# Loads through one queue in order of use, keys turned after the values' second product, and the maxima split for both query blocks at once

## The chip, the cores and the metric

The program runs on one core of a Trainium2 chip. The time is that of one execution on the device, in microseconds (us); the number compared is the median of several runs. A core has a matrix engine (PE, with its weight loads, PEld, shown beside it), a vector engine (DVE), a scalar engine (ACT), a general engine (POOL) and a sequencer (SP) that issues transfers. Each engine works through its own instructions in order; transfers run on 16 shared DMA engines, fed from a queue of SP and a queue of ACT.

## The reference

Eight sequences of 256 rows and 512 columns go through four residual steps, each with a layer norm in front and the tanh of a gate as factor. Cut to what matters here:

```python
x = x + tanh(g_xattn[0]) * causal_attention(layernorm(x), ctx, ctx)     # 16 heads of 32, keys = values = context
x = x + tanh(g_ffn[0])   * ternary_ffn(layernorm(x))                    # weights quantized per group of 64, in bf16
x = x + tanh(g_xattn[1]) * cross_attention(layernorm(x), ctx)           # q, k, v, o linears; q and k normed by their rms
x = x + tanh(g_ffn[1])   * bit_ffn(layernorm(x))                        # 8-bit activations, ternary weights
```

The second attention takes its keys and values from the context through `k_img_w` and `v_img_w`: `k = rms_norm(ctx @ k_w.T + k_b)`, `v = ctx @ v_w.T + v_b`. They don't depend on x. Both attentions need a maximum per query row and head before their exponentials.

## The kernel before

The work is in three stages. In the first (lines 819 to 861) the kernel quantizes the weights of the first feed-forward, computes the keys and values of the second attention for all eight sequences and parks them in device memory, and does the first attention of the sequences 0 and 1. In the second (1123 to 1162) PE runs the first feed-forward of all sequences, with the other attentions between its chunks. In the third (1365 to 1391) it runs the second feed-forward with the remaining cross attentions.

**The written order.** Each piece of work is a step with a place on a time axis, and `timeline` (617) emits the steps in order of their places. In the first stage one unit of the axis is one unit of weights (a block of 128 x 1024), and three units go with one sequence's keys and values. PE keeps this order exactly, since `pe.held` chains its instructions (860). The other engines and the queues don't: the framework orders their instructions by its own estimate of when each becomes ready, earlier places first among those that are ready, and adds the waits. `behind` (301) pins an instruction after a named one.

**A unit u of weights** (`quantize0`, 701): `sizes` at u - 0.5 starts the load of unit u + 1 and has ACT write the absolute values `a` and the signs `sg` (716); `mean(0)` at u is a product on PE into the one bank of `mean`, copied out by ACT into `s` (724); `rest` at u + 0.45 is the second such product and five instructions of DVE (736 to 740). The loads of units go into two buffers, so unit 2 can only be loaded when the signs of unit 0 are done.

**A sequence b of keys and values** (`keys_values`, 790): `load` of the turned context `cT`; `k0` and `k1`, two linears of eight records on PE, each with the bias `rkb` added by DVE and squared by ACT (756, 757); `scale`, where POOL takes the root (274) and scales the two halves (764); `turn`, eight transposes on PE into a pair of banks and a copy of 1024 columns by ACT (348); `store` of the keys (803); `v0` and `v1`, the values' linears with the bias `rvb` (810), the second followed by the store of the values (812). Its places within the three units are in lines 845 to 849: k0 0.1 (for sequence 0 at -0.6), k1 0.85, scale 0.9, v0 1.6, turn 2.15, store 2.16, v1 2.35.

**The first attention of sequences 0 and 1** (850 to 857) has its steps at 0.5, 1.25 and 2.75 of each three units: the turn of its queries `y` (569), four `scores` (385), whose row maxima `nm` are reduced by DVE (412), then `parts` (423), `shift` (443), four `exps` (451) and four `weigh` (488). `parts` splits each maximum into three bf16 terms in the tile `mz`, in POOL: per query block q and term k a copy that rounds and, but for the last term, a subtraction, ten instructions on 16 values per partition. `shift` turns `mz` on PE (tile `nt`, 447) and DVE copies it to `nT` (449), which `exps` uses as an operand. `scores`, `exps` and `turned` share the two pairs of banks of tag `s`.

**The first loads** (826 to 834): SP issues `cT` of sequence 0, units 0 and 1, `wv` (1 MB) and the rows x0 and x1; ACT issues the gates, the four blocks of `wk` and the broadcast rows `rkb` and `rvb`, before its first computations. Behind these SP issues, in the order that the framework chose, the first attentions' `kT` and `v`, the next `cT`, x2 and x3, and unit 2.

**Into the second stage**: the rows x4 to x15 are loaded into a pool that takes the place of the first stage's buffers, so these loads wait until the tiles beneath are free. Sequence 2's layer norm (`norm`, 563) reads x4 and x5; `layernorm` pins its DVE statistics (281) behind the last product with the up half that was emitted before it (912). Its place is 1.4 of the first 16 chunks (line 1153), between chunks 1 and 2; its turn is at 4.2. A chunk is `hidden` (892): 32 products into a bank `gu`, of which there are two, then ACT's tanh, two DVE instructions (911, 912), a cast and a subtraction for the low half; `project` (927) follows three chunks later.

Of the kernel before, what the change touches and what calls it, by code (L numbers as in the profile page):

```python
# [45 lines left out]
ALU = mybir.AluOpType  # L46
# [4 lines left out]
P = 128  # L51
# [26 lines left out]
MP = 3  # L78
# [9 lines left out]
def flamingo_kernel(  # L88
# [273 lines left out]
    class Attention:  # L362
# [60 lines left out]
        def parts(self):  # L423

            part = self.mz.rearrange("p q (r k g) -> p k r q g", r=4, g=DC)
            rest = small.tile([P, 4, 2, DC], F32, tag="nmr", name="nmr", bufs=2)
            src = self.nm
            for k in range(MP):
                for q in range(2):
                    if k + 1 < MP:  # L430
                        nc.gpsimd.tensor_scalar(
                            part[:, k, :, q], src[:, :, q], 1.0, 0.0, ALU.mult, ALU.add
                        )
                        nc.gpsimd.tensor_tensor(
                            rest[:, :, q], src[:, :, q], part[:, k, :, q], ALU.subtract
                        )
                    else:
                        nc.gpsimd.tensor_scalar(
                            part[:, k, :, q], src[:, :, q], 1.0, 0.0, ALU.mult, ALU.add
                        )  # L440
                src = rest

        def shift(self):
# [163 lines left out]
    def load_w(pool, name, wT):  # L607
        w = pool.tile([P, DC, D], F32, tag=f"w{name}", name=f"w{name}", bufs=1)
        nc.sync.dma_start(out=w, in_=wT.rearrange("(c p) o -> p c o", p=P))
        return w  # L610

    def load_row(pool, name, row, tag=None, bufs=1):
        t = pool.tile([P, D], F32, tag=tag or f"r{name}", name=f"r{name}", bufs=bufs)
        nc.scalar.dma_start(out=t, in_=row.partition_broadcast(P))
        return t

    def timeline(*jobs):
# [202 lines left out]
    with ExitStack() as part:  # L820
# [4 lines left out]
        wk = [prep.tile([P, D], F32, tag=f"wk{c}", name=f"wk{c}") for c in range(DC)]  # L825
        kv[0][0]()
        for c in range(DC):
            nc.scalar.dma_start(out=wk[c], in_=k_wT[c * P : (c + 1) * P, :])
        for u in range(AHEAD + 1):
            load0(u, prep)  # L830
        rkb, rvb = load_row(prep, "kb", k_b), load_row(prep, "vb", v_b)
        wv = load_w(prep, "v", v_wT)
        load_x(0, x0)
        load_x(1, x0)

# [5 lines left out]
        for b in range(B):  # L841
            load, k0, k1, scale, turn, store, v0, v1 = kv[b]
            if b:
                jobs += on((3 * b - 2, load))
            jobs += on(
                *((3 * b + n, f) for n, f in zip(
                    (0.1 if b else -0.6, 0.85, 0.9, 2.15, 2.16, 1.6, 2.35), (k0, k1, scale, turn, store, v0, v1)
                ))
            )
        for a, n in zip(att0, (0, 12)):  # L850
            places = [n + 3 * k + f for k in range(5) for f in (0.5, 1.25, 2.75)]
            jobs += on(*zip((n + 0.3, n + 0.35, places[2]), a.ready()))
# [270 lines left out]
    with ExitStack() as part:  # L1123
# [320 lines left out]
```

## Time and profile before

| | |
|---|---|
| median of 3 runs | 1199.13 us (1198.99 to 1200.08) |
| the profiled execution's own time | 1195.64 us |
| its span, first to last instruction | 1193.9 us |
| PE busy | 1091.6 us (91%) |
| DVE busy | 789.3 us (66%) |
| ACT busy | 595.2 us (50%) |
| POOL busy | 503.2 us (42%) |
| granted PE clock, mean | 0.987 |

Times in the profile count from the first instruction. The first stage runs to about 196 us. A linear of 512 columns shows as eight records of 0.43 us; PE's ends are modelled, so waits are read from the idle time that stands in brackets before an instruction, with what ended it. A broad share of the whole says little here, since the stages have different limits; the rows of the stretch in question do.

### The profile page before, as it was taken

The numbers are of one execution on the slowest core, as the hardware profiler recorded it, in microseconds if no ns is written. First come the engines' busy times: TensorE is split into PE (matmuls) and PEld (weight loads), VectorE is DVE, ScalarE is ACT, GpSimd is POOL, SyncE is SP. The second block draws the span as 40 slices with busy tenths as digits, with TensorE's granted clock in tenths as the row PEclk, the third lists the DMA queues.
The fourth block names the chain that finished last, engine by engine and source line by source line (L and its number), as shares of the span: only waits on it lengthen the run. The fifth ranks groups of instructions, "written<-read, shape, count | busy, mean of one in ns | idle before, by whom it ended". The sixth has DMA issues, their size and how long they took to land.

```text
span 1193.9 us, 31314 instructions
## 1 busy us (share of the span) xinstructions
PE 1091.6 (91%) x13290; PEld 737.9 (62%) x13389; DVE 789.3 (66%) x1612; ACT 595.2 (50%) x1058; POOL 503.2 (42%) x794
## 2 busy tenths in 40 slices
PE   5899998999999988988899998898999999999986
PEld 1445446777777666766677776565656565656653
DVE  5786986745546374655646445786868686868586
ACT  3566554565665443344344442546364636464663
POOL 3113013433435474575544326544444444424251
PEclk9999999999999999999999999999999999999999
DMA  8444436423333232333211014012121212211212
GB/s 299 144 171 150 168 112 209 129 92 120 97 123 81 86 83 89 100 89 103 64 49 42 19 37 159 18 47 51 49 50 50 49 50 50 54 32 32 42 39 59
DMA packets 99469, 104.08 MB, mean 87 GB/s; under 512 B 60992, under 2 KB 72320, under 8 KB 99328
## 3 DMA queue, kind: packets, MB, share of 16 engines
q1 hardware_dynamic: 95728, 96.03, 27.4%
q10 hardware_dynamic: 3600, 6.03, 1.5%
q8 instruction: 105, 1.72, 0.6%
q14 instruction: 36, 0.29, 0.1%
HBM read 72.09 MB, written 15.73 MB: 74 GB/s over the span
## 4 chain that ended last, share of the span: by engine, by line
PE 35%; DVE 30%; POOL 15%; ACT 11%; issue 7%; DMA 3%; DVEq 0%; SPq 0%; POOLq 0%; ACTq 0%
PE gu L257 9%; PE lin L257 6%; PE o L257 6%; PE s L257 5%; DVE nm L419 4%; PE y L257 3%; ACT h L919 2%; DVE h L912 2%; POOL hs L299 2%; POOL rs_r L274 2%; DVE u L1276 2%; POOL acc L921 2%; DVE h L911 2%; PE py L257 2%; DVE ln_st L281 2%
## 5 line engine op out<-in xcount | busy, mean ns | idle before, releaser
L257 PE MATMUL gu<-xT,gu 128*128 128x128 f16 x4096 | 255.1, 221 | 9.6 <-DMA xT<-yp 5.8
L257 PEld LDWEIGHTS <-gu 128*128 128x128 bf16 x4096 | 237.7, 99 | 40.3 <-issue 19.4
L257 PE MATMUL gu<-gv,zT 128*128 128x256 fp8e4 x1024 | 131.1, 274 | 11.9 <-DMA zT<-zq 7.0
L274 POOL TENSOR_TENSOR rs_r<-rs_t,mhalf 128x1 f32<-128x1 f32 (+1 forms) x88 | 60.1, 687 | 181.1 <-DVE rs_t L272 161.6
L921 POOL TENSOR_TENSOR acc<-acc,h 128x256 f32<-128x256 f32 x112 | 82.5, 736 | 117.5 <-ACT h L919 108.4
L257 PEld LDWEIGHTS <-zT 128*128 128x128 bf16 x1024 | 96.1, 98 | 57.6 <-issue 35.4
L1269 ACT COPY gv<-gu 128x512 f32<-128x512 f32 x128 | 74.0, 585 | 110.1 <-PE gu L257 90.9
L916 ACT CAST hs<-h 128x256 f16<-128x256 f32 x128 | 51.7, 404 | 143.1 <-DVE h L912 142.2
L911 DVE SCALAR_TENSOR_TENSOR h<-h,gu 128x256 f32<-128x256 f32 x128 | 53.1, 415 | 103.2 <-ACT h L910 103.1
L257 PE MATMUL y<-pr,hs 128*128 128x512 bf16 x413 | 113.5, 383 | 6.9 <-DVE x L963 1.0
L485 ACT ACTIVATE p<-s 128x768 f32<-128x768 f32 (+1 forms) x128 | 109.6, 907 | 18.1 <-PE s L257 18.0
L419 DVE TENSOR_REDUCE nm<-s 128x4 f32<-128x1024 f32 x64 | 75.7, 1218 | 34.4 <-PE s L257 34.4
L919 ACT ACTIVATE h<-h,hid 128x256 f32<-128x256 f32 x112 | 56.7, 507 | 68.5 <-POOL hs L299 42.9
L299 POOL TENSOR_TENSOR hs<-h,hs 128x256 f16<-128x256 f32 x64 | 44.9, 702 | 99.8 <-ACT hs L916 99.8
L522 POOL TENSOR_TENSOR oT<-oT 128x128 f32<-128x128 f32 x48 | 24.1, 502 | 138.7 <-ACT oT L519 136.1
L257 PE MATMUL s<-qT,kT 32*128 32x256 f32 (+1 forms) x1024 | 76.8, 375 | 3.7 <-DVE rs_t L272 2.1
L910 ACT ACTIVATE h<-gu 128x256 f32<-128x256 f32 x128 | 48.5, 379 | 49.7 <-PE gu L257 49.3
L1274 DVE SCALAR_TENSOR_TENSOR t<-t,gv 128x512 f32<-128x512 f32 x64 | 46.9, 733 | 39.5 <-ACT t L1273 39.5
L257 PE MATMUL s<-kT,qT 32*128 32x256 f32 (+1 forms) x1024 | 69.5, 377 | 2.0 <-ACT p L485 1.7
L257 PE MATMUL lin<-wk,cT 128*128 128x512 f32 x128 | 60.0, 612 | 9.8 <-DMA wk<-in_k_wT_dram 9.8
L411 DVE TENSOR_REDUCE nm<-s 128x2 f32<-128x256 f32 (+1 forms) x128 | 62.8, 550 | 7.5 <-PE s L257 7.5
L257 PEld LDWEIGHTS <-hs 128*128 128x128 f16 x512 | 46.2, 101 | 34.2 <-issue 3.4
(181 smaller groups left out, 2097.7 us busy)
## 6 DMA issues: line engine op xcount, KB each, us to landing
w<-in_gvT_dram SPq DMA_DIRECT2D x32, 512.0 KB
w<-in_guT_dram SPq DMA_DIRECT2D x16, 512.0 KB
w<-in_outT_dram SPq DMA_DIRECT2D x16, 512.0 KB
cT<-in_cxT_dram SPq DMA_DIRECT2D x8, 512.0 KB
x<-in_x_dram SPq DMA_DIRECT2D x16, 256.0 KB
kT<-in_cxT_dram SPq DMA_DIRECT2D x8, 512.0 KB
v<-in_cx_dram SPq DMA_DIRECT2D x8, 512.0 KB
kd<-k SPq DMA_DIRECT2D x8, 512.0 KB
```

What stands on the lines that cost most here:

```text
L257: return self.kept(nc.tensor.matmul(*args, **kwargs))
L274: nc.gpsimd.tensor_tensor(r[:, :n], t[:, :n], mhalf[:, :n], ALU.pow)
L299: (nc.vector if engine == "V" else nc.gpsimd).tensor_tensor(dst, a, b, op)
L411: nc.vector.tensor_reduce(nm[:, :, qb], s[j][:, :, at[qb] : at[qb] + to[qb]], AX.X, ALU.max, negate=True,)
L419: nc.vector.tensor_reduce(nm, s[j].rearrange("p r (q k) -> p r q k", q=2), AX.X, ALU.max, negate=True)
L485: exp[0] = nc.scalar.activation(self.p[j], s[j][:, :, 0:n], AF.Exp)
L910: block["A"] = nc.scalar.activation(h, gu[:, 0], AF.Tanh, scale=0.5 / UP0)
L911: nc.vector.scalar_tensor_tensor(h, h, 1.0, gu[:, 0], ALU.add, ALU.mult)
L916: nc.scalar.copy(hs[:, 0], h)
L919: nc.scalar.activation(sq, h, AF.Square, scale=hid[:, 1:2])
L921: block["P"] = nc.gpsimd.tensor_tensor(self.acc[i], self.acc[i], sq, ALU.add)
L1269: nc.scalar.copy(self.gv[:, :, k % 2, :], gu)
```

## The change

It has three named parts and some places that move with them.

First loads: `wk`, `rkb` and `rvb` go from ACT's queue to SP's, and SP's order becomes cT, wk (4 blocks), unit 0, rkb, unit 1, wv, rvb, x0, x1. ACT issues only the gates.

Keys: `turn` and `store` move from 2.15 and 2.16 to 2.75 and 2.76, behind `v1` at 2.35. The attention's step at 2.75 moves to 2.15, between v0 and v1. `shift` moves from 7.7 to 7.5, that is, from behind v0 to in front of it.

Parts: the loop over q goes; each copy and subtraction covers both query blocks (32 values per partition), five instructions instead of ten. This holds for all 16 attentions.

Besides, sequence 2's norm moves from 1.4 to 2.4, behind chunk 2.

```diff
             for k in range(MP):
-                for q in range(2):
-                    if k + 1 < MP:
-                        nc.gpsimd.tensor_scalar(
-                            part[:, k, :, q], src[:, :, q], 1.0, 0.0, ALU.mult, ALU.add
-                        )
-                        nc.gpsimd.tensor_tensor(
-                            rest[:, :, q], src[:, :, q], part[:, k, :, q], ALU.subtract
-                        )
-                    else:
...
+                nc.gpsimd.tensor_scalar(part[:, k], src, 1.0, 0.0, ALU.mult, ALU.add)
+                if k + 1 < MP:
+                    nc.gpsimd.tensor_tensor(rest, src, part[:, k], ALU.subtract)
                 src = rest
...
-    def load_row(pool, name, row, tag=None, bufs=1):
+    def load_row(pool, name, row, tag=None, bufs=1, queue=nc.scalar):
...
-        nc.scalar.dma_start(out=t, in_=row.partition_broadcast(P))
+        queue.dma_start(out=t, in_=row.partition_broadcast(P))
...
         for c in range(DC):
-            nc.scalar.dma_start(out=wk[c], in_=k_wT[c * P : (c + 1) * P, :])
-        for u in range(AHEAD + 1):
-            load0(u, prep)
-        rkb, rvb = load_row(prep, "kb", k_b), load_row(prep, "vb", v_b)
+            nc.sync.dma_start(out=wk[c], in_=k_wT[c * P : (c + 1) * P, :])
+        load0(0, prep)
+        rkb = load_row(prep, "kb", k_b, queue=nc.sync)
+        load0(1, prep)
         wv = load_w(prep, "v", v_wT)
+        rvb = load_row(prep, "vb", v_b, queue=nc.sync)
         load_x(0, x0)
         load_x(1, x0)
...
-                    (0.1 if b else -0.6, 0.85, 0.9, 2.15, 2.16, 1.6, 2.35), (k0, k1, scale, turn, store, v0, v1)
+                    (0.1 if b else -0.6, 0.85, 0.9, 2.75, 2.76, 1.6, 2.35), (k0, k1, scale, turn, store, v0, v1)
...
-            places = [n + 3 * k + f for k in range(5) for f in (0.5, 1.25, 2.75)]
+            places = [n + 3 * k + f for k in range(5) for f in (0.5, 1.25, 2.15)]
             jobs += on(*zip((n + 0.3, n + 0.35, places[2]), a.ready()))
-            jobs += on(*zip((*places[3:7], places[6] + 0.1, n + 7.7), a.looks()))
+            jobs += on(*zip((*places[3:7], places[6] + 0.1, n + 7.5), a.looks()))
...
-                jobs += at(n, *zip((-4.8, *((1.4, 4.2) if n == 0 else (-2.4, 0.2))), a.ready()))
+                jobs += at(n, *zip((-4.8, *((2.4, 4.2) if n == 0 else (-2.4, 0.2))), a.ready()))
```

More of the change, by code (lines that the diff above doesn't have):

```diff
@@ L428, in parts @@
             for k in range(MP):
-                for q in range(2):
-                    if k + 1 < MP:
-                        nc.gpsimd.tensor_scalar(
-                            part[:, k, :, q], src[:, :, q], 1.0, 0.0, ALU.mult, ALU.add
-                        )
-                        nc.gpsimd.tensor_tensor(
-                            rest[:, :, q], src[:, :, q], part[:, k, :, q], ALU.subtract
-                        )
-                    else:
-                        nc.gpsimd.tensor_scalar(
-                            part[:, k, :, q], src[:, :, q], 1.0, 0.0, ALU.mult, ALU.add
-                        )
+                nc.gpsimd.tensor_scalar(part[:, k], src, 1.0, 0.0, ALU.mult, ALU.add)
+                if k + 1 < MP:
+                    nc.gpsimd.tensor_tensor(rest, src, part[:, k], ALU.subtract)
                 src = rest
```

## The prediction

> **What bounds the kernel now.** I read the page's totals first, then the busy time in stretches of 20 us, then what PE waits for inside the first stage, then the timeline around each wait. All edits but the parts lie before 213 us.
>
> Page, totals, and stretches of 20 us (busy us of each engine, clock, transfers):
>
> ```profile
> PE 1091.6 (91%) x13290; PEld 737.9 (62%) x13389; DVE 789.3 (66%) x1612; ACT 595.2 (50%) x1058; POOL 503.2 (42%) x794
> ...
> 0.00:20.00 20.00, 9.37 (x18) 3.70 (x19) 8.62 (x36) 4.55 (x6) 6.37 (x34) 1.00 0.82 297
> 20.00:40.00 20.00, 13.72 (x41) 6.51 (x41) 14.19 (x23) 11.27 (x18) 5.18 (x5) 0.91 0.65 223
> 40.00:60.00 20.00, 18.55 (x141) 8.89 (x140) 17.24 (x27) 11.35 (x19) 2.05 (x3) 1.00 0.41 145
> 120.00:140.00 20.00, 17.87 (x109) 8.34 (x108) 18.92 (x35) 11.47 (x17) 2.05 (x3) 1.00 0.45 149
> ```
>
> PE is the bound from 40 us on, with DVE close behind where scores are reduced (18.92 of 20). Before 40 us PE is busy for 23.1 of 40: the gain to be had is there. Next PE's own waits from 14 to 205 us, and the timeline of the start (PE, SP's queue, ACT):
>
> ```profile
> PE mean L257 <- ACT a L716: 7.3, 9, 1.9
> PE turned L260 <- POOL lin L764: 4.6, 6, 2.3
> PE mean L257 <- ACT s L724: 2.8, 4, 1.0
> ```
>
> ```profile
> 9.79 5.34 PE L257 MATMUL lin<-wk,cT 128*128 128x512 f32 x8 [9.79 <-DMA wk<-in_k_wT_dram]
> ...
> 23.37 5.29 PE L257 MATMUL lin<-wv,cT 128*128 128x512 f32 x8
> 28.49 0.38 PE L257 MATMUL mean<-a,blk 128*128 128x512 bf16 x1
> 31.18 0.66 PE L260 MATMUL turned<-ident,lin 128*128 128x128 f32 x4 [2.31 <-POOL lin L764]
> 32.28 0.66 PE L260 MATMUL turned<-ident,lin 128*128 128x128 f32 x4 [0.44 <-POOL lin L764]
> ```
>
> ```profile
> 19.45 0.39 SPq L696 DMA_DIRECT2D w<-in_guT_dram  x1
> ```
>
> ```profile
> 27.29 1.06 ACT L716 ACTIVATE a<-w 128x1024 bf16<-128x1024 f32 x1 [0.82 <-DMA w<-in_guT_dram]
> ```
>
> The first product starts at 9.79, paced by wk. Unit 2 is issued at 19.45, behind seven other loads, and lands at 27.29; its first mean follows at 28.49, whatever PE did before. Then the turn of the keys waits 2.31 + 0.44 us for POOL. In half-microsecond stretches the transfers run at 350 to 420 GB/s from 6.5 to 27.5 us: the whole prologue is limited by the order in which bytes come. Last, the passage into the second stage, DVE and PE:
>
> ```profile
> 202.62 1.33 DVE L281 BATCH_NORM_STATS2 ln_st<-x 128x6 f32<-128x512 f32 x2 [1.11 <-DMA x<-in_x_dram]
> ```
>
> ```profile
> 207.51 3.47 PE L257 MATMUL gu<-xT,gu 128*128 128x128 f16 x32 [2.33 <-DVE h L912]
> ```
>
> The statistics wait for x4 and hold up line 912 behind them, PE idles 2.33 us and then runs 32 products in 3.47 us instead of the 1.8 to 1.9 of the later ones: clock, 0.77 in that stretch (205 to 210).
>
> **First loads.** 0.53 MB are in by 6.0 us (sum of the rows), then about 395 GB/s. Checked on before: the 4.72 MB up to x1 give 6.0 + 10.6 = 16.6, and DVE's first statistics start at 16.92, so a landing costs 0.3 more. The new order by the same rule: cT 6, wk 7.0 to 9.0 (0.66 each), unit 0 10.3, rkb 11.0, unit 1 12.3, wv 15.0, x1 17.0. PE: k0 ends at 9.9 (9.0 plus two records of 0.43) instead of 15.1; a of unit 0 10.3 to 11.4; the two means at 11.5 and 13.05, with sg (1.04) and the copy (0.6) between; k1 13.3 to 16.8; means of unit 1 at 16.8 and 17.9; v0 18.1 to 21.5. ACT no longer issues six loads before its first a (which started at 11.49, right after the last of them), and DVE's k0 bias no longer stands behind x.
>
> Then unit 2 decides. All bytes ahead of it are the same, so if it keeps its place it lands at 27.2 again: its mean stays at 28.49, after 7 us without PE work. From there the new order is turn of y 0.87, v1 3.44, 0.22 for the mean: second mean of unit 2 at 33.0, before 36.21, a gain of 3.2. After idling PE loses clock: before, v0 ran at 0.50 (23.5 to 26.5) and took 5.29, not the 3.59 of the other linears, so 1.7 comes off: gain 1.5. If unit 2 moves up, it gains what is passed. Its buffer comes free with sg of unit 0, and ACT starts this unit without six issues ahead, while SP has six more of its own to issue (0.33 to 0.5 each); so I take it that fewer of the later loads are ready to be put in front of it, and that x2, x3 and the second attention's kT and v (1.57 MB, 4.0 us; needed some 80 us later) fall behind. Then: landing 23.2, mean 24.4, second mean 24.4 + 4.5 + 1.7 = 30.6: **-5.6**. Directly behind kT and v, with warm clock, it is -8.8 (landing 21.7, mean 22.9, second mean 27.4); unchanged -1.5; a queue that stalls could bring +2. SP issues six more, 2.4 us, under transfers that are behind anyway.
>
> [...]
>
> **Keys' turn behind v1**, from the second sequence on. The waits for POOL at 73.65 and 161.36 go (0.93 + 0.92): -1.85. What is late next is a of the next unit: second mean, copy 0.6, a 1.06, first mean take 2.01 us in every period where the fill is short (36.21 to 38.22, 57.12 to 59.13, and so on). The fill was the attention's step and is now the turn of 1.1 us, so each of seven periods waits 0.76 as those with the turn of y did, 5.3 for 3.9: +1.5. One wait of the last weighing goes (0.60 at 194.56). ACT's copy of the keys (1.01) then follows sg, under k0; the store of keys moves past the value store on SP, and nothing there waits but the end of the stage (below).
>
> **Shift in front of v0.** Before, the maxima are done about 68.8 and the parts occupy POOL from 68.78 to 71.41, hidden by v0 (68.99 to 72.42):
>
> ```profile
> 68.78 0.20 POOL L431 TENSOR_SCALAR mz<-nm 128x16 bf16<-128x16 f32 x1 [16.42 <-DVE nm L411]
> ...
> 71.21 0.20 POOL L438 TENSOR_SCALAR mz<-nmr 128x16 bf16<-128x16 f32 x1
> ```
>
> Starts of dependent steps are 0.3 apart, and a step on 32 values costs little more than 16 (0.50 for 128, 0.20 to 0.22 for 16), so five take 1.6: ready at 70.4 and visible at 70.6. PE wants them at 69.0, since DVE is full up to there: 1.6 twice (the second at 156.5), +3.2, less 0.3 of a wait absorbed. Bounds: 0 if the earlier third score moves DVE's work enough; 3.5 each if also nT's copy stands behind the five instructions of a unit, as it did at 76.36. Together with the turn: **+2.0** (-2.5 to +6).
>
> **Norm behind chunk 2.** DVE goes from 912 of chunk 1 at 201.6 to the attention's ending and on to 912 of chunk 2 by 205.3 instead of 207.45, so PE's 2.33 idle and the 1.6 of slow clock can go. Against it: the turn of y at 208.3 wants statistics, root and two y (4.3 us after x). And x lands later: the stage's key store now follows v1, at about 195 instead of 191.29, and if the rows' buffers wait for it, x4 comes at 204 to 206.5. Between -4 and +3 (x at 209); I take **-1.5**.
>
> **Parts in the other attentions.** 2.25 us become 1.6 in six, 1.75 become 1.5 in eight: 5.9 us of POOL, of which PE sees few, the chain of waits going through POOL for 15%: **-0.6** (-3 to 0). [...] By spans, ten of 0.20 to 0.22 fall to five, 1.05 us saved each, and by starts 0.25 to 0.65; the starts decide.
>
> **Sum**: -5.6 + 2.0 - 1.5 - 0.6 = -5.7 us. Against the profiled execution, 1195.64 (span 1193.9 and 1.7 around it), that is 1189.9; the median of the runs lies 3.5 above the profiled one, so I predict 1199.1 - 5.7, **1193.4**.
>
> **Rivals.**
> A, unit 2 keeps its place: -1.5 + 2.0 - 1.5 - 0.6 = -1.6, 1197.5. For it: seven loads stood ready before it and nothing in the edit pins the order. Against: ACT's earlier start.
> B, slower, the maxima come too late: at 69 and 157 us PE waits for the parts, and again in the first exps for nT behind DVE's five instructions, 3.5 twice instead of 1.6, with a clock loss of 1.7 each: 7.2 more than the sum has, +1.5, and 1200.6; with a unit 2 in its old place 1204.7. It decides once each place costs PE over 5.7 / 2 + 1.6 = 4.5 us. For it: DVE at 18.9 of 20. Against: DVE is free for some 1.6 us soon after, at 78.88.
> C, the loads do more than I count, -8.8, and the passage loses both its wait and its clock, -3: 1199.1 - 8.8 + 2.0 - 3 - 0.6 = 1188.7.
>
> **How the numbers follow.** Forecast 0.38 (its own range 1191 to 1196), A 0.27, B 0.2, C 0.15. 1187 to 1202 leaves out the outer parts of B and C. About 0.2%, 2.4 us, is what a measurement can tell from no change: A is split by it (0.09 faster, 0.16 same, 0.02 slower), forecast and C are faster but for 0.02, B is 0.04 same and 0.16 slower. Faster 0.60, same 0.22, slower 0.18.
>
> **What would show it.** First product near 7 us; a of unit 2 near 23; second mean of unit 2 near 30.6; no wait of the turn on POOL, a wait of about 0.76 of each first mean of a third unit, a new wait of nt on POOL of 1.6; five POOL instructions per attention; 912 of chunk 2 not behind the statistics. I am wrong if unit 2 lands at 27 again, if nT holds up the exps, or if the framework's new order on DVE and ACT moves waits into the later stages, which this sum holds at nothing but the parts.

## The result

The change makes the kernel slower: 1202.78 us median of 16 runs (1198.1 to 1206.9) against 1199.06 of 16 runs of the kernel before (1195.1 to 1201.2) on the same chips. The ratio is 1.0038, with a 95% interval of 1.0026 to 1.0051. The profiled execution of the changed kernel took 1205.13 us (span 1203.4, before 1193.9), so 9.5 us of span are to be found, more than the 3.7 between the medians: the profiled execution before was 3.4 us faster than its median, that of the changed kernel 2.4 slower. Its mean granted clock was 0.979, before 0.987. Over the 16 runs, a clock of 0.977 to 0.978 goes with 1206 to 1207 us and one of 0.984 with 1198 to 1201.

The profile of the changed kernel: first PE's totals on the page, then the busy time of the engines in stretches of 20 us (columns: stretch, its length, PE, PEld, DVE, ACT, POOL busy, granted clock, share of the transfer engines, GB/s), then what PE waited for between 14 and 225 us.

```profile
PE 1101.0 (91%) x13290; PEld 742.6 (62%) x13389; DVE 795.2 (66%) x1612; ACT 595.6 (49%) x1058; POOL 491.1 (41%) x714
```

```profile
0.00:20.00 20.00, 10.94 (x22) 4.65 (x23) 11.12 (x36) 8.01 (x12) 5.46 (x32) 1.00 0.81 296
20.00:40.00 20.00, 15.09 (x43) 7.67 (x42) 11.97 (x25) 8.34 (x12) 4.65 (x6) 0.83 0.68 239
```

```profile
PE mean L257 <- ACT a L707: 10.6, 9, 4.2
PE turned L260 <- POOL y L294: 5.1, 1, 5.1
PE nt L260 <- POOL mz L429: 3.6, 2, 1.8
PE s L257 <- DVE nm L411: 3.2, 3, 1.9
```

PE executes the same number of matmuls as before (13290) and is busy for 9.4 us longer, while over the whole span it is idle for as long as before (102.4 and 102.3 us): the same work took longer. The granted clock in these two traces is either full (1.00) or half (0.50); half was granted for 30.7 us in all before and for 51.2 after, and 20.5 us more at half clock are some 10 us of work, about the whole difference.

The waits have moved. The turn's waits for POOL's `lin` (4.6 us) and `gu`'s wait of 2.33 for h are gone or smaller. In their place stand a wait of 4.2 us for the weights of unit 2, two for the parts of the maxima (`mz`), a longer one for the maxima (`nm`), and one of 5.1 us for the `y` of sequence 2. PE's timeline at these places shows what follows the waits (the wait and its releaser stand in brackets):

```profile
27.22 0.59 PE L257 MATMUL mean<-a,blk 128*128 128x512 bf16 x1 [4.16 <-ACT a L707]
...
29.31 5.34 PE L257 MATMUL lin<-wv,cT 128*128 128x512 f32 x8
34.48 0.38 PE L257 MATMUL mean<-a,blk 128*128 128x512 bf16 x1
...
69.39 0.29 PE L260 MATMUL nt<-ident_b,mz 128*128 128x128 bf16 x2 [1.82 <-POOL mz L429]
69.51 5.35 PE L257 MATMUL lin<-wv,cT 128*128 128x512 f32 x8
...
138.54 0.36 PE L257 MATMUL s<-mask_q_m,mask_q_f 32*128 32x64 bf16 x14 [1.93 <-DVE nm L411]
138.66 1.67 PE L257 MATMUL s<-kT,qT 32*128 32x128 f32 x16
...
163.56 0.29 PE L260 MATMUL nt<-ident_b,mz 128*128 128x128 bf16 x2 [1.82 <-POOL mz L429]
...
218.88 1.97 PE L260 MATMUL turned<-ident,y 128*128 128x128 f32 x8 [5.05 <-POOL y L294]
220.63 3.54 PE L257 MATMUL gu<-xT,gu 128*128 128x128 f16 x32
```

A linear of eight f32 products takes 3.59 to 3.70 us at full clock, and 5.34 and 5.35 here; 32 `gu` products take 1.95 and here 3.54. The clock granted in these stretches shows why: 0.50 from 29.5 to 32.5 us, 0.50 from 70.35 to 73.77, from 138.62 to 142.03 and from 219 to 223, but 1.00 behind the second `nt` (163.8 to 167). So a wait is paid twice in four of these five places: once as idle time, and again in products at half clock behind it.

The account of the 9.5 us, from the moments at which the same instruction starts in both profiles (firsts are the first means of the units 3, 6, 9 and so on, which stand at the boundaries of the sequences):

| stretch on PE | before | after | difference |
|---|---|---|---|
| start to second mean of unit 2 | 36.21 | 34.48 | -1.73 |
| to first of unit 6 | 22.92 | 23.20 | +0.28 |
| first of 6 to 9 (wait for `mz`) | 21.56 | 24.00 | +2.44 |
| 9 to 12 | 24.02 | 25.04 | +1.02 |
| 12 to 15 | 20.33 | 20.31 | -0.02 |
| 15 to 18 (wait for `nm`) | 21.50 | 24.57 | +3.07 |
| 18 to 21 (wait for `mz`) | 21.86 | 22.56 | +0.70 |
| 21 to first `gu` | 27.61 | 27.14 | -0.47 |
| first `gu` to turn of `y` | 15.79 | 17.58 | +1.79 |
| turn of `y` to an addition in the first block of stage two (232.8, 242.3) | 21.0 | 23.4 | +2.4 |

These add up to 9.5, and from there to the end both kernels take 961.1 us. Up to that addition PE is idle for 3.5 us longer than before and busy for 6.0 longer.

### The profile page after: what moved, and what is told of

Read it like the earlier page. It is cut to its first block, busy times and chain, and to the rows that moved or that the text cites. A ratio compares the mean times of both kernels' runs of the same rounds, so it can differ in the third digit from the quotient of the medians.

```text
span 1203.4 us, 31222 instructions
## 1 busy us (share of the span) xinstructions
PE 1101.0 (91%) x13290; PEld 742.6 (62%) x13389; DVE 795.2 (66%) x1612; ACT 595.6 (49%) x1058; POOL 491.1 (41%) x714
## 3 DMA queue, kind: packets, MB, share of 16 engines
q8 instruction: 105, 1.72, 0.6%
## 4 chain that ended last, share of the span: by engine, by line
PE 42%; DVE 28%; POOL 11%; ACT 10%; issue 5%; DMA 3%; DVEq 0%; POOLq 0%; SPq 0%; ACTq 0%
PE gu L257 11%; PE lin L257 8%; PE s L257 6%; PE o L257 6%; PE y L257 3%; DVE nm L419 3%; DVE u L1268 2%; DVE h L904 2%; ACT h L911 2%; PE proj L257 2%; PE py L257 2%; POOL hs L299 2%; DVE h L903 2%; POOL acc L913 2%; DVE t L1266 2%
## 5 line engine op out<-in xcount | busy, mean ns | idle before, releaser
L257 PEld LDWEIGHTS <-zT 128*128 128x128 bf16 x1024 | 95.8, 98 | 55.3 <-issue 36.7
L476 ACT ACTIVATE p<-s 128x768 f32<-128x768 f32 (+1 forms) x128 | 109.5, 906 | 17.7 <-PE s L257 17.6
L257 PE MATMUL o<-p,v 128*32 128x256 f32 (+1 forms) x1024 | 61.7, 358 | 5.7 <-DVE x L1298 4.3
```

Of the source, the lines that this page charges most:

```text
L257: return self.kept(nc.tensor.matmul(*args, **kwargs))
L476: exp[0] = nc.scalar.activation(self.p[j], s[j][:, :, 0:n], AF.Exp)
```

## The experiments

Every ratio is against the kernel before, on the same chip, with its 95% interval; a median stands against the 1197.8 to 1199.2 of the kernel before in the same series. "Second mean" is that of unit 2 on PE (36.21 before, 34.48 changed).

### The four parts alone

**e1_loads**, the first loads only:

```
-            nc.scalar.dma_start(out=wk[c], in_=k_wT[c * P : (c + 1) * P, :])
-        for u in range(AHEAD + 1):
-            load0(u, prep)
-        rkb, rvb = load_row(prep, "kb", k_b), load_row(prep, "vb", v_b)
+            nc.sync.dma_start(out=wk[c], in_=k_wT[c * P : (c + 1) * P, :])
+        load0(0, prep)
+        rkb = load_row(prep, "kb", k_b, queue=nc.sync)
+        load0(1, prep)
         wv = load_w(prep, "v", v_wT)
+        rvb = load_row(prep, "vb", v_b, queue=nc.sync)
```

> The kernel before with the new first loads alone. Theory T (each part has its own place and price, as the traces before and after show): the start gains as in the changed kernel, the second mean of unit 2 at 34 to 35 us instead of 36.2, so 1 to 3 us faster in all. Rival R (the loss is mostly clock: more stretches at half clock, wherever they fall, and no part has a price of its own): within 1 us of before.

Measured: 1194.73, ratio 0.9972 (0.9956 to 0.9988), faster. The second mean is at 34.37, 1.84 earlier. ACT's first step on unit 2 ends its wait with the transfer:

```profile
26.04 1.06 ACT L716 ACTIVATE a<-w 128x1024 bf16<-128x1024 f32 x1 [0.54 <-DMA w<-in_guT_dram]
```

So unit 2 lands at 26.0, not at 23.2, and the loads alone are worth some 3 us in the median. That the second mean shows only 1.84 of them is a matter of the one profile before: with its loads and its places at the start, the second mean stood at 37.22 in e4_norm and at 37.82 in e3_parts. A gain read at the start from one pair of profiles is uncertain by some 1.5 us.

**e2_turn**, the keys' turn and store, y's turn and the shift:

```
-(0.1 if b else -0.6, 0.85, 0.9, 2.15, 2.16, 1.6, 2.35)
+(0.1 if b else -0.6, 0.85, 0.9, 2.75, 2.76, 1.6, 2.35)
-for f in (0.5, 1.25, 2.75)]
+for f in (0.5, 1.25, 2.15)]
-n + 7.7), a.looks()
+n + 7.5), a.looks()
```

> The kernel before with the keys' turn, the attention's places and the shift moved, with the old ten-step parts and the old norm. Theory T: two waits of nt on the parts, longer than after's 1.82 us since ten steps take 2.6 (2.5 to 3 each), a longer wait of the scores for the maxima in the second attention (about 2.9 us lost between the first means of units 15 and 18), seven waits of 0.76 for a; the first stage ends 5 to 8 us later and the kernel is 4 to 8 us slower. Rival R: within 2 us of before.

Measured: 1205.57, ratio 1.0061 (1.0039 to 1.0084), slower. The second mean is at 33.29, 2.9 earlier and with no half clock; then each stretch with attention work loses: +0.9 from the first of 6 to 9, +1.0 from 9 to 12, +1.6 from 15 to 18, +2.1 from 18 to 21. The parts, with the old ten instructions, come late for both halves of nt:

```profile
67.61 0.23 PE L260 MATMUL nt<-ident_b,mz 128*128 128x128 bf16 x1 [1.23 <-POOL mz L438]
68.38 0.23 PE L260 MATMUL nt<-ident_b,mz 128*128 128x128 bf16 x1 [0.53 <-POOL mz L438]
```

Together that is 1.76 us, not the 2.5 to 3 that T expected, and no more than the 1.82 with five instructions. POOL's first copy shows why, here and in the changed kernel:

```profile
65.69 0.20 POOL L431 TENSOR_SCALAR mz<-nm 128x16 bf16<-128x16 f32 x1 [16.24 <-DVE nm L411]
```

```profile
67.47 0.58 POOL L429 TENSOR_SCALAR mz<-nm 128x32 bf16<-128x32 f32 x1 [16.83 <-DVE nm L411]
```

DVE reduces the last two maxima one behind the other, from 65.18 to 66.19 here and from 66.36 to 67.38 in the changed kernel. The copy of one query block starts behind the first of them, the copy of both only behind the second. From the start of the two reductions to the end of PE's last wait for `mz` it takes 3.20 us with ten instructions and 3.03 with five.

**e3_parts**, the five instructions in place of ten:

```
+                nc.gpsimd.tensor_scalar(part[:, k], src, 1.0, 0.0, ALU.mult, ALU.add)
+                if k + 1 < MP:
+                    nc.gpsimd.tensor_tensor(rest, src, part[:, k], ALU.subtract)
```

> The kernel before with five-step parts alone. Theory T: POOL is off PE's path in the first stage except at the turns of units 8 and 20, which wait 0.9 us for POOL in before; up to 2 us faster there, and 0 to 1 us in the later stages: 0 to 3 us faster. Rival R: within 1 us.

Measured: 1198.98, ratio 1.0009 (0.9994 to 1.0024): no difference. The keys' turn still waits 0.49 and 0.44 us for POOL (at 75.25 and 76.34), as before; what POOL waits for there is the root's operand from DVE (`rs_t`, 72.93), not the parts, so the gain that T expected did not come.

**e4_norm**, the norm of sequence 2:

```
-*((1.4, 4.2) if n == 0 else (-2.4, 0.2))
+*((2.4, 4.2) if n == 0 else (-2.4, 0.2))
```

> The kernel before with sequence 2's norm behind chunk 2 alone. Theory T, as the changed kernel shows it (statistics behind 912 of chunk 2, root and y late on POOL, the queries' turn waits 5.05 us and PE falls to half clock): 2 to 5 us slower, the turn waiting for y. Rival R3 (the late statistics are only bad because the rows land later when the keys' store stands behind v1): here the rows land as before, PE's idle of 2.33 us before chunk 4 goes, the turn waits under 1.5 us, and the kernel is 1 to 3 us faster.

Measured: 1204.35, ratio 1.0046 (1.0025 to 1.0066), slower. The first statistics wait for no rows, and the idle time of 2.33 us before `gu` is gone. DVE (statistics), POOL (`y`) and PE (turn) in this run:

```profile
205.75 1.28 DVE L281 BATCH_NORM_STATS2 ln_st<-x 128x6 f32<-128x512 f32 x2
206.94 0.40 DVE L911 SCALAR_TENSOR_TENSOR h<-h,gu 128x256 f32<-128x256 f32 x1
207.26 1.28 DVE L281 BATCH_NORM_STATS2 ln_st<-x 128x6 f32<-128x512 f32 x2
...
210.21 0.15 DVE L272 TENSOR_SCALAR rs_t<-ln_mv 128x2 f32<-128x2 f32 x1
```

```profile
210.85 1.36 POOL L274 TENSOR_TENSOR rs_r<-rs_t,mhalf 128x2 f32<-128x2 f32 x2
...
212.89 3.01 POOL L294 TENSOR_SCALAR y<-x,ln_mv,rs_r 128x512 f32<-128x512 f32 x4
```

```profile
213.71 1.97 PE L260 MATMUL turned<-ident,y 128*128 128x128 f32 x8 [4.91 <-POOL y L294]
215.47 3.55 PE L257 MATMUL gu<-xT,gu 128*128 128x128 f16 x32
```

Moved to this place, the norm meets another norm: four statistics, two roots and four `y` instead of two, one and two, with instructions of h between them. Before, the two stood apart (statistics at 202.62 and 207.70, `y` at 207.95 and 212.65), and the turn at 211.80 found its `y` ready. From the start of the statistics to the first `y` at 213.64 it takes 7.9 us. The wait of 2.3 has become one of 4.9, with half clock behind. As the rows are there in time, the cause is not that x lands late. From the first `gu` to the addition of the table's last row it takes 40.2 us instead of 36.7. The profiled execution is the fastest of the twelve (1196.54); its 3.4 us of loss in the passage are made up behind it, so where the rest of the 5.5 in the median lies is not shown.

### Undoing one part

**e5_shift_back**, the changed kernel with the shift where it was:

```
-            jobs += on(*zip((*places[3:7], places[6] + 0.1, n + 7.5), a.looks()))
+            jobs += on(*zip((*places[3:7], places[6] + 0.1, n + 7.7), a.looks()))
```

> The changed kernel with the shift of the maxima back at unit 7.7. Theory T (each moved step has its own place and its own price): the two transposes nt, which wait 1.82 us each for the parts on POOL (mz, L429), find their operands ready, so 2 x 1.82 go, and what the clock loses just behind them (v0 5.35 us instead of 3.6) goes too; against this the exponentials may wait for the transposes. Time 2 to 4 us under the changed kernel's 1202.8, so about 1199 to 1201; the stretch between the first means of unit 6 and unit 9 falls back from 24.0 to about 22. Theory R (what the clock happens to grant sets the result): within 1 us of the changed kernel.

Measured: 1211.73, ratio 1.0122 (1.0094 to 1.015). Theory T had the sign wrong: the kernel is 9 us slower still.

```profile
70.66 0.28 PE L260 MATMUL nt<-ident_b,mz 128*128 128x128 bf16 x2
...
74.59 0.40 PE L257 MATMUL s<-mask_k_m,mask_k_f 32*128 32x64 bf16 x14 [3.31 <-DVE nT L440]
...
76.68 5.46 PE L257 MATMUL lin<-wv,cT 128*128 128x512 f32 x8
```

The transposes have their operands, but the scores that use nT now follow 0.4 us behind them and wait 3.31 for its copy on DVE, in both attentions. Before the change the keys' turn, a mean and v1 lay in between. The loss is the turn's: it took this cover away. The earlier shift does not cause a loss; it turns a wait of 3.31 into one of 1.82.

**e6_norm_back**, the changed kernel with the norm at 1.4 again:

```
-*((2.4, 4.2) if n == 0 else (-2.4, 0.2))
+*((1.4, 4.2) if n == 0 else (-2.4, 0.2))
```

> The changed kernel with the first norm of sequence 2 back at 1.4 of its chunk. Theory T: the 5.05 us for which the turn of y waits for POOL go, and with them the half clock behind (1.97 instead of 1.04 for the turn, 3.54 instead of 1.9 for gu); in their place gu waits for h, 0.5 and 2.6 us, as in the run that has only the turn, the places and the shift. Time 2 to 5 us under the changed kernel's 1202.8, so 1198 to 1201. Theory R: within 1 us of the changed kernel. If the norm's loss depends on how late the rows of sequence 2 land, the passage from gu to the turn of y (17.6 us in the changed kernel, 15.8 before) falls only to 17.

Measured: 1200.83, ratio 1.0013 (0.9994 to 1.0032), 2 us under the changed kernel, at the edge of what T expected. The wait of 5.05 is gone and `gu` waits for h instead, 3.2 us in two places, as T had it; but the half clock did not go, as the `gu` behind the longer of them (2.63 us) took 3.37. The passage from the first `gu` to the turn took 16.6 us, below the 17.0 named for the case that late rows matter; and though SP issues x at 201.75 in the changed kernel (193.29 before), its statistics at 210.79 show no wait for a transfer.

**e9_store_late**, one DMA moved on SP:

```
-(0.1 if b else -0.6, 0.85, 0.9, 2.75, 2.76, 1.6, 2.35)
+(0.1 if b else -0.6, 0.85, 0.9, 2.75, 3.6 if b == 4 else 2.76, 1.6, 2.35)
...
-                    nc.sync.dma_start(
+                    late[0] = nc.sync.dma_start(
                         out=smax[4 * u + 2 * k : 4 * u + 2 * k + 2, :],
...
-            nc.sync.dma_start(out=kd1[b], in_=st["k"].rearrange("p c t -> p (c t)"))
+            behind(nc.sync.dma_start(out=kd1[b], in_=st["k"].rearrange("p c t -> p (c t)")),
+                   late[0] if b == 4 else None)
```

> The changed kernel with one thing moved: the store of sequence 4's turned keys is issued on SP behind the last pair of smax stores of unit 15 instead of just ahead of them; every other instruction stands as it did. Theory S (the 1.93 us for which the scores of unit 16 wait is the store's doing: it takes the rings ahead of the last smax store, top's reduction waits 1.07 us for that, and nm stands behind it on DVE): top waits for nothing, the scores wait 1.4 as before the change, the stretch from the first mean of unit 15 to that of unit 18 falls from 24.6 to 21.5 to 22.5, and the time by 1 to 3 us against the changed kernel's 1202.8. Rival (top is late by its own data, and half the clock there comes of the granted clock alone): top's wait stays within 0.3 of 1.07, the time within 1.

Measured: 1201.53, ratio 1.0024 (1.0011 to 1.0037). DVE's `top` and PE's scores in unit 16:

```profile
133.52 0.68 DVE L658 TENSOR_REDUCE top<-smax 64x1 f32<-64x512 bf16 x1 [0.32 <-issue]
```

```profile
137.31 0.29 PE L257 MATMUL s<-mask_q_m,mask_q_f 32*128 32x64 bf16 x14 [1.77 <-DVE nm L411]
...
139.21 4.53 PE L257 MATMUL lin<-wv,cT 128*128 128x512 f32 x8
```

The store did make `top` late (1.07 became 0.32), but that is only 0.16 of the scores' wait, 1.93 to 1.77; the stretch took 23.8 us and not 21.5 to 22.5. Theory S falls as the explanation of the 3 us. Most of them lie behind the wait, at half clock. Nor does it take the keys' turn: e12_start_nopin (below) has the old order in this stretch and shows a wait of 1.73 us, half clock behind it and 23.55 us; e8_start a wait of 1.76 at full clock and 21.88.

**e10_old_at_shift**, the old order in the two sequences with a shift:

```
-(0.1 if b else -0.6, 0.85, 0.9, 2.75, 2.76, 1.6, 2.35)
+(0.1 if b else -0.6, 0.85, 0.9, *((2.15, 2.16) if b in (2, 6) else (2.75, 2.76)), 1.6, 2.35)
-for f in (0.5, 1.25, 2.15)]
+for f in (0.5, 1.25, 2.75 if k == 2 else 2.15)]
-n + 7.5), a.looks()
+n + 7.7), a.looks()
```

> The changed kernel with the old order in the two sequences in which the maxima are shifted, 2 and 6: there the keys turn at 2.15 behind the values' first linear, y at 2.75, and the shift stands at 7.7 and 19.7 again; the other six sequences keep the change. Theory T (what the changed kernel loses in these sequences is the work that lay between nt and the scores that use nT: 3.6 us of waits and the half clock behind the first of them): no wait for mz or nT above 0.7, the stretch from the first mean of unit 6 to that of unit 9 at 21.5 to 22 instead of 24.0, the time 3 to 5 us under the changed kernel's 1202.8: 1198 to 1200. Rival (the clock takes the time somewhere else): the stretch falls, the time stays within 1.

Measured: 1204.05 (1195.3 to 1209.7), ratio 1.0038 (1.0015 to 1.0062), no better than the changed kernel. The stretch from the first of 6 to 9 did fall, from 24.0 to 21.1, with no wait for `mz` or nT. The rival's words fit the whole: the stretch falls, the time stays. In this run's profile the scores of unit 16 were followed by products at half clock (v0 5.60 us) and the stretch from 15 to 18 took 26.1; from stage two on 7 more came (+6.6 against before at the first block's addition, +13.6 in stage three). Behind that addition half clock was granted for 45 us, against 24 before and 31 in the changed kernel. The runs of this kernel lie 14 us apart, with clocks from 0.987 (1195.3) to 0.973 (1209.7).

### Is the idle PE the cause of the half clock?

The profiles of before, of the changed kernel and of fourteen experiments allow a count of PE's waits between 60 and 200 us. Behind the waits of 1.36 and 1.37 us for `nm` (five profiles) the next linear took 3.60 in all five. Of 17 waits of 1.72 to 1.93, 11 were followed by a linear of 4.28 to 5.61 and 6 by one of 3.60 to 3.65, at the same places. Behind both waits of 3.31 the linear took 5.4 to 5.5, and behind the ten of 4.2 to 5.2 at the start 4.5 to 5.3. The waits of 1.23 and 0.5 close together in e2_turn were followed once by 3.65 and once by 4.93. Length alone does not decide, then. A count is not a cause either, so two runs filled waits with work whose results are overwritten.

**e13_fill_nt** and **e14_fill_both**, added to the changed kernel:

```
             t = pair((P, 2, P), BF, name="nt")
+            for _ in range(18 if self.causal and self.b < 2 else 0):
+                pe.transpose(t[:, 0, :], ident_b, ident_b)
```

and, in e14_fill_both alone, for the turn of sequence 2's y:

```
         t = pair((P, 2, DC, P), name="turned")
+        for _ in range(fill):
+            pe.transpose(t[:, 0, 0, :], ident, ident)
```

> The changed kernel with 18 transposes of the identity, whose results are overwritten, put on PE ahead of the transposes nt of attention 0 and 1, where PE waits 1.82 us for mz. They fill some 1.2 us of that wait; nothing that the kernel needs comes earlier. Theory C (the half clock behind the wait comes of PE's idle time): v0 behind the first nt takes 3.6 to 3.7 us instead of 5.35 though nt itself is no earlier, the stretch from the first mean of unit 6 to that of unit 9 falls from 24.0 to 22.0 to 22.6, the mean granted clock rises, and the time falls by 1 to 2 us against the changed kernel's 1202.8. Rival (the clock falls at these places for another reason, such as the transfers or the maxima's work beside it): v0 at 5.35 again, stretch and time as in the changed kernel or 1 us longer.

> As the run that fills the wait for mz, and 32 further transposes of the identity ahead of the turn of sequence 2's y, where PE waits 5.05 us for POOL: some 4.2 us of that wait. Theory C: the turn takes 1.04 us instead of 1.97 and the gu behind it 1.95 instead of 3.54, with the turn's own start where it was (17.6 us behind the first gu); 2 to 3 us more than the filled nt alone gives. Rival: both stay at twice their length, or the 32 transposes end behind the moment at which y is there and the turn starts later.

PE in e13_fill_nt, then in e14_fill_both:

```profile
67.36 1.17 PE L260 MATMUL nt<-ident_b 128*128 128x128 bf16 x18
69.34 0.28 PE L260 MATMUL nt<-ident_b,mz 128*128 128x128 bf16 x2 [0.82 <-POOL mz L429]
69.46 3.65 PE L257 MATMUL lin<-wv,cT 128*128 128x512 f32 x8
```

```profile
212.79 3.66 PE L260 MATMUL turned<-ident 128*128 128x128 f32 x32
218.03 1.41 PE L260 MATMUL turned<-ident,y 128*128 128x128 f32 x8 [1.58 <-POOL y L294]
219.27 1.95 PE L257 MATMUL gu<-xT,gu 128*128 128x128 f16 x32
```

nt starts where it did (69.34 for 69.39), and v0 behind it takes 3.65 instead of 5.35; the stretch falls from 24.0 to 22.3. In e14 the turn starts 17.6 us behind the first `gu` as in the changed kernel, takes 1.41 (1.04 was expected, 1.97 stood before) and `gu` 1.95 instead of 3.54; behind the six unfilled waits of 4.9 to 5.1 for `y` in other profiles `gu` took 3.1 to 3.6. All four filled waits for `mz` in the two runs are followed by 3.65, four of the six unfilled by 5.35. At these places theory C holds: where the idle time was filled, the half clock did not come.

What differs between a wait that half clock follows and an equal one that it does not follow can be seen in the granted clock of the profiles of before and of the changed kernel. In both, all its changes are whole multiples of 3.41 us apart: in the changed kernel half clock begins up to 245 us at 25.98, 70.35, 138.62 and 217.12, which are 13, 20 and 23 times 3.41 apart, and it lasts 3.41 or 6.83. PE's busy time in the windows of 3.41 us between these moments, at the two waits of 1.82 (columns as above):

```profile
66.94:70.35 3.41, 1.34 (x5) 0.56 (x5) 2.27 (x6) 1.88 (x5) 1.70 (x6) 1.00 0.05 19
70.35:73.77 3.42, 3.42 (x5) 1.35 (x4) 3.27 (x4) 1.42 (x2) 3.32 (x3) 0.50 0.25 74
...
159.10:162.51 3.41, 2.27 (x8) 0.79 (x6) 3.41 (x7) 0.58 (x1) 0.79 (x2) 1.00 0.46 154
162.51:165.92 3.41, 2.36 (x8) 1.16 (x9) 2.53 (x8) 3.08 (x5) 2.32 (x5) 1.00 0.00 0
```

The first wait falls, with the end of one of 0.67, into one window, in which PE is busy for 1.34 of 3.41 us, and the next window is at half clock. The second, just as long, is divided by a boundary, with PE busy for 2.27 and 2.36 us, and the clock stays at 1.00. From 14 to 245 us the two profiles have 125 such windows at full clock: the six with PE busy for 0.03 to 0.39 of the window were followed by half clock, and none of the 119 others, with 0.58 or more. Behind 245 us the share alone does not separate them: of 540 windows, the 14 that half clock followed had 0.26 to 0.57, and 11 that it did not follow had 0.43 to 0.55. Against the first instruction the windows lie differently in the two profiles: 25.98, where half clock begins in the changed kernel, and 23.36 before are 2.62 us apart.

The whole did not follow: 1205.57 (ratio 1.0061, 1.0038 to 1.0083) and 1208.46 (1.0089, 1.007 to 1.0108), 3 and 6 us above the changed kernel where 1 to 2 and 3 to 5 less were expected. The extra instructions also changed the order of some 30 instructions of DVE in e13 and 60 in e14, and of some of ACT and SP, so these kernels are no pure tests of the total. The profiled run of e13 is 2.5 us shorter in span than that of the changed kernel (1200.9): the filled stretch gives 1.7 of it, and 1.6 come from the stretch from 15 to 18, where the wait of 1.93, unfilled, happened to stay at full clock. Where its other runs lose more is not shown.

### What the start needs

**e7_unit2**, the kernel before with the first loads and with loads that nothing needs yet queued behind that of unit 2 (each of x 2 and 3, the next cT, attention 1's kT and v in the same way):

```
+            if u == 2:
+                late[0] = ins
...
-        nc.sync.dma_start(out=xs[i], in_=xf[i * P : (i + 1) * P, :])
+        behind(nc.sync.dma_start(out=xs[i], in_=xf[i * P : (i + 1) * P, :]), late[0])
```

> The kernel before with the first loads of the change, and in addition the loads of x 2 and 3, of the next context and of attention 1's keys and values queued behind the load of unit 2. Theory T (the landing of unit 2 is what holds the start, because loads that nothing needs yet are in front of it): unit 2 lands at 20.5 to 22 instead of 26.0, the wait of its mean goes, and the next wait is that of the keys' turn for POOL; second mean of unit 2 at 31 to 33.5 instead of 34.4, time 1 to 3 us under that of the first loads alone (1194.7). Rival (what holds the start is the transfers' rate, not their order): unit 2's mean stays at 26 to 27 and the time within 0.5 of the first loads alone.

**e8_start**, and in addition the turn of the keys behind v1 in sequence 0 alone:

```
-(0.1 if b else -0.6, 0.85, 0.9, 2.15, 2.16, 1.6, 2.35)
+(0.1 if b else -0.6, 0.85, 0.9, *((2.15, 2.16) if b else (2.75, 2.76)), 1.6, 2.35)
-            jobs += on(*zip((n + 0.3, n + 0.35, places[2]), a.ready()))
+            jobs += on(*zip((n + 0.3, n + 0.35, places[2] if n else 2.15), a.ready()))
```

> The kernel of the run with unit 2 ahead, and in addition the keys' turn of sequence 0 alone at 2.75 (store 2.76) and y's turn of sequence 0 at 2.15; the other sequences, the shift, the parts and the norm as before. Theory T (the turn behind v1 is good at the start, where POOL's bias comes late, and bad later, where the keys wait for nothing): second mean of unit 2 at 27.5 to 30, all later stretches as before, time 1188 to 1192, the fastest of all. Rival (the half clock behind an idle PE takes back what the start gains): second mean of unit 2 at 30 or later, the time within 1 us of the run with unit 2 ahead alone.

**e12_start_nopin**, e8_start without the loads queued behind unit 2's:

```
-            if u == 2:
-                late[0] = ins
```

> The kernel of the run e8_start without the loads queued behind unit 2's: the first loads of the change, and the keys' turn at 2.75 and y's at 2.15 in sequence 0 alone. Theory T (both are needed at the start: with unit 2 landing at 26 PE idles some 4 us and v1 runs at half clock, as in the changed kernel): second mean of unit 2 at 33.5 to 34.5, the time 1193 to 1195.5, 3 to 5 us above e8_start. Rival (the turn's place alone does it): second mean of unit 2 at 31 or earlier, the time within 1.5 us of e8_start.

PE in e7_unit2, in e8_start, and in e12_start_nopin:

```profile
29.02 1.97 PE L262 MATMUL turned<-ident,lin 128*128 128x128 f32 x8 [5.16 <-POOL lin L772]
30.78 5.16 PE L259 MATMUL lin<-wv,cT 128*128 128x512 f32 x8
35.78 0.38 PE L259 MATMUL mean<-a,blk 128*128 128x512 bf16 x1
```

```profile
22.90 0.38 PE L259 MATMUL mean<-a,blk 128*128 128x512 bf16 x1 [0.44 <-ACT a L724]
24.30 1.41 PE L262 MATMUL turned<-ident,y 128*128 128x128 f32 x8 [1.02 <-POOL y L296]
25.54 3.60 PE L259 MATMUL lin<-wv,cT 128*128 128x512 f32 x8
28.98 0.38 PE L259 MATMUL mean<-a,blk 128*128 128x512 bf16 x1
```

```profile
27.15 0.59 PE L257 MATMUL mean<-a,blk 128*128 128x512 bf16 x1 [4.29 <-ACT a L716]
...
29.23 5.20 PE L257 MATMUL lin<-wv,cT 128*128 128x512 f32 x8
```

With the order pinned, unit 2 lands at 21.8 instead of 26.0. That alone gains nothing over the loads (1196.65, ratio 0.9978, 0.996 to 0.9996): PE comes sooner to the keys' turn and waits 5.16 there for POOL, at half clock afterwards; T had expected 31 to 33.5; it named this wait, but not its length and its half clock. The turn alone, on top of the loads, gains nothing either (1194.18, ratio 0.9965, 0.995 to 0.998; second mean 34.27, as T had it). Both together take the second mean to 28.98, 7.2 us earlier than before, and leave no half clock there (v1 takes 3.60): **1190.74, ratio 0.994 (0.9916 to 0.9964)**, some 8 us faster than the kernel before and the fastest version here.

**e11_norm_turn**, e8_start with the norm at 2.4 and what depends on it later:

```
-*((1.4, 4.2) if n == 0
+*((2.4, 6.2) if n == 0
-*((5.4, 7.2) if n == 0
+*((7.4, 8.4) if n == 0
```

> The kernel of the run e8_start with the norm of sequence 2 at 2.4, as in the change, and with it the turn of y at 6.2 instead of 4.2 and its first two scores at 7.4 and 8.4 instead of 5.4 and 7.2. Theory T (the norm's loss is that the turn stands where it stood, 4.3 us behind statistics that now take 7.9 to reach the first half of y): gu does not wait for h, the turn waits less than 1 us, and the time is 1 to 3 us under that of e8_start (1190.7), or the same if the scores are late instead. Rival (the norm's statistics are bad at that place whatever stands behind them, as they keep DVE from h): 3 us or more above e8_start.

Measured: 1194.78, ratio 0.996 (0.9943 to 0.9977), 4 above e8_start. The turn, at 207.84, waits for nothing and the two waits for h are 1.4 together, but the scores are late:

```profile
217.81 0.20 PE L259 MATMUL s<-mask_q_m,mask_q_f 32*128 32x64 bf16 x2 [2.57 <-DVE nm L413]
218.75 0.29 PE L259 MATMUL s<-mask_q_m,mask_q_f 32*128 32x64 bf16 x14 [0.73 <-DVE nm L413]
...
219.97 3.28 PE L259 MATMUL gu<-xT,gu 128*128 128x128 f16 x32
```

The wait has moved once more, and the half clock with it. Theory T allowed late scores but not their price.

## Why the prediction was wrong

It said 1193.4, faster, in a range of 1187 to 1202; the time lies just above that range. For -5.6 at the start, +2.0 for turn and shift, -1.5 for the norm and -0.6 for the parts, the two profiles show -1.73, +7.0, +4.2 and nothing behind the addition. The terms, one by one:

- **First loads, -5.6: mis-sized.** First product at 7.71 for "near 7", ACT's earlier start and the order up to x1 came as worked out. The step that failed is "fewer of the later loads are ready to be put in front of" unit 2. SP issued it at 16.99, behind cT, x 2 and 3 and attention 1's kT; it was moved past one load, and its first step on ACT ran at 26.11, not 23.2. Only rival A had this, and its term for the start, -1.5, is close to the measured -1.73 (against the starts of e3 and e4, which have the old loads too, the gain is 2.7 to 3.3). The bound of -8.8 is what e8_start reaches (-7.2) once the order is pinned.
- **Keys' turn, +1.5 - 1.85 = -0.35: the mechanism was right, the rest was not seen.** The turn's waits on POOL are gone, and waits of 0.75 to 0.76 stand at the first means, as forecast; the stretches to unit 6 and from 9 to 12 lose 0.28 and 1.02. What the term left out is that the turn was the cover between nt and the scores that use nT (e5_shift_back: 3.31 us twice without the earlier shift).
- **Shift, +3.2: right in the wait, short in the price.** 1.6 was forecast for each nt and 1.82 measured. "The maxima are done about 68.8" read POOL's first copy, which needs one query block; the second block's maxima were done at 69.30, and the merged copy waits for both (e2_turn). The 1.7 us at half clock behind the first was in rival B alone. The scores of unit 16, where the stretch lost 3.07, were in no term; the store of keys was named as harmless on SP, and moving it back changed `top` by 0.75 us and the scores by 0.16. The group had +2.0 in the sum; alone, with a gain of 2.9 at the start, it measured 1.0061, some +7 us.
- **Norm, -1.5: wrong in sign.** The idle time before `gu` did go. The failed step is "the turn of y at 208.3 wants statistics, root and two y (4.3 us after x)": it took 7.9 to the first `y`, since another norm's statistics and roots came between. Before, with the two norms apart, it had taken 6.1 to the first `y` and 6.8 to the second (202.62 to 208.7 and 209.5), so 4.3 was too little by the rows at hand. Alone it measured 1.0046; taking it out of the changed kernel gave back 2 us.
- **Parts, -0.6**: no difference measured, within what was said. In front of v0 the five instructions gained 0.17 us over ten.
- **Added terms.** The four parts alone come to -0.28 + 0.61 + 0.09 + 0.46 = +0.88%, and together they give +0.38%. By the four intervals the sum is uncertain by 0.4, so the difference is only just clear of noise; a reason for it is that the parts share waits. The start is the plain case: 1.84 from the loads and 2.9 from the turn become 1.73, as unit 2 lands when it did and PE only idles for longer.

Rival B, slower through the maxima, was the nearest: its 1204.7 with unit 2 in its old place is 2 above the measured median, and its price for a place, a wait with 1.7 us of lost clock, is what the first nt shows. Its second wait, for nT, came only without the earlier shift. So the closeness of its number is in part luck: the two stretches with nt lost 2.44 and 0.70, and the scores of unit 16 and the norm, which it did not name, 3.07 and 4.2.

What stays open: the local gains of e10, e13 and e14 (1.7 to 3 us) are seen in their stretches and not in their medians. The order of work in the later stages differs between these kernels, and so does the clock there; which of these takes the time is not settled. Why the runs of one kernel differ in their clock (0.977 to 0.984 in the changed kernel) is not shown either, since each kernel has one profile.

## What to carry to other kernels

A step that one engine is waited for in may itself be the cover for the next dependence: before moving it, list the pairs of producer and consumer that it stood between. Price a new wait of PE together with the products behind it: here, the wait of 1.82 us at 69.39 was followed by 3.41 us at half clock, some 1.7 us of lost work on top of the wait, and the equal one at 163.56 by none. Look at neighbouring short waits together: in e3_parts waits of 1.06 and 1.04 us stood before the means at 22.32 and 23.73, and the next linear took 5.29, while in e4_norm 1.37 and 1.04 at the same two means left it at 3.59. Where an order of transfers is worth microseconds, pin it, and look at the wait that comes next: neither the order nor the turn gained alone what both gained together.

## What the runs showed of the hardware that was not expected

- In the profiles of before and of the changed kernel PE's granted clock was 1.00 or 0.50, with all changes whole multiples of 3.41 us apart. From 14 to 245 us the six of 125 windows of full clock that half clock followed had PE busy for 0.03 to 0.39, the others for 0.58 or more; behind 245 us the 14 of 540 had 0.26 to 0.57, with 11 others at 0.43 to 0.55. Behind 14 us, full clock came back after 20 of 24 windows at half clock, in which PE was busy for 0.93 or more, and not after the other four, with 0.49 to 0.86.
- Idle time of 1.72 to 1.93 us on PE between 60 and 200 us was followed by a linear of 4.28 to 5.61 us in 11 of 17 cases and by one of 3.60 to 3.65 in six; 1.36 and 1.37 us by 3.60 in all five; 3.31 us there and 4.2 to 5.2 at the start by 4.5 to 5.5 in all twelve. Throwaway transposes in the gap (1.17 us of a wait that was 1.82) kept v0 at 3.65 in four of four cases, where six unfilled ones gave 5.35 four times.
- The runs of one kernel, e10_old_at_shift, lie 14 us apart (1195.3 to 1209.7), largely in step with the mean granted clock (0.987 to 0.973).
